# Two layers of attention and experts on one core: the first and last steps of attention prepared by half quarters, between the groups of the half before

## The chip, the core and the metric

The kernel runs on one core of a Trainium2 chip. The metric is the time of one execution on the device in microseconds, and less is better. TensorE multiplies matrices and transposes; VectorE does the elementwise work, the maxima and the reductions; ScalarE does activations and copies; GpSimd (POOL in the profile) does elementwise work beside them and issues the indirect DMAs; SyncE (SP) issues most of the other DMAs. [...]

## The reference

The input `x` has 16 x 256 rows of 128 numbers in f32. All arithmetic is f32. Cut to what matters:

```python
x = L0_attn_a_x                                    # (16, 256, 128)
x = x + attn_a(layernorm(x))    # 16 heads of 8, softmax within blocks of 64 along axis 1
x = x + ffn(layernorm(x))
x = x + attn_b(layernorm(x))    # linear, 16 heads of 8 along axis 0 (16 long), with a bias, linear
x = x + ffn(layernorm(x))

def ffn(x):                                        # 8 experts, hidden 512
    top_vals, top_idx = top_k(flat_x @ Wr, 2)
    combine = the softmax of top_vals, put at top_idx, zero elsewhere
    h = silu(flat_x Wg[e]) * (flat_x Wu[e])
    return sum over e of combine[e] * (h Wd[e]) / sqrt(12)
```

`attn_b` adds to its scores a bias that is 1 on the diagonal and beside it, around the ring of 16. The kernel computes an expert only for the rows that chose it.

## The kernel before, in words

**Tiling.** The 256 positions are cut into four quarters of 64 (`NQ`); a quarter is 1024 rows, held in the tile `xq[q]` as eight groups (`NG`) of 128 rows. `CH` is half a quarter, 512 rows. "Layer 0" is attention A and the experts behind it, "layer 1" is attention B and the experts behind that.

**Attention A** (`attention_a`, L345) takes one quarter. First comes the preparation of the whole quarter: `layernorm_t` (L249) takes the statistics of eight groups on VectorE (L253), the inverse root as a `pow` on GpSimd (`rs`, L258), normalizes on VectorE (L266) and transposes on TensorE (L270); then `queries` (L287), one matmul and four scaled copies on ScalarE (L293) for each half, and `keys` (L297), one matmul, a copy (L302) and four masked products on VectorE (L304). Then the eight groups run one after the other: values (L320), scores (L374), maxima and subtraction on VectorE (L382, L383), the exponential on ScalarE (L388), transposes (L393) with their copies (L397), the product with the values (L404), the division on VectorE (`divided`, L334), and on GpSimd the bias of the values and the addition to `xq` (L411, L412).

**Attention B** (`attention_b`, L416) does the same over the other axis, two groups at a time, with a linear map `xt` (L437) before the queries and keys. Its layernorm writes one tile `lnT` of the whole quarter, because it regroups the rows by position. Behind each group's division stand a transpose of its output (`ot`, L507) and a copy into `oT` (L508); when all eight groups are done two output products `y` (L518) are added to `xq`.

**Router** (L530), one for each quarter and layer: layernorm, logits (L544), the two largest, and the place of each row among those of its expert (L607 to L615). Then 16 indirect DMAs on GpSimd (L640), the *scatters*, put the rows, with their weight and place, into a table in DRAM that is sorted by expert. `tile_tables` works out, on VectorE, which tiles of 256 rows of one expert are full by now.

**Experts** (`experts`, L796): 39 tiles for each layer, in lists of 9, 8 and 22 that become known after the routers of quarters 1, 2 and 3. `fetch` (L797) issues on SyncE the load of a tile's 256 rows (`xin`) and three weights of 256 KB each, two tiles ahead. A *unit* is half a tile: matmuls `g` and `u` (L891), tanh on ScalarE (L896), two products on VectorE (L897, L899), and `down` (L838), the second matmuls `acc` of the unit before. Behind a tile its results are put to DRAM by two indirect DMAs on GpSimd (L864). There are 79 units for each layer (`UNITS`).

**Combine** (L913): for half a quarter, one load (`back`) on SyncE (L917), which waits for the results of all tiles that can hold rows of that quarter, and two additions on VectorE (L927). It stands ahead of attention B in layer 1, and behind everything at the end, where the sums go to the output.

**What sets the order.** The generators yield after each step, and the program's main loop (from L958) interleaves them; a tile scheduler then orders each engine's queue by the program and by buffers. A router runs in every second step of the attention of the quarter that follows (L978 to L980). `beside` (L958) spreads expert units over an attention: those of layer 0 over quarters 0 to 2 of layer 1, and 9 (`BESIDE`) of its own layer over quarter 3 of each layer. The rest of the experts run after quarter 3. `follow(put_row, before[layer] + beat)` (L647) makes each scatter wait for a recent instruction of the attention (`beat`), so that they are paced. The PSUM pool `mm` has two buffers, which transposes, queries, keys, values, outputs and `y` share; scores have two of their own, the experts three and one.

**Loads** (L147 to L173). SyncE: `x` of quarter 0, then of quarter 1, the weights of attention B, then `x` of quarters 2 and 3. ScalarE: `k_sb`, all constants in one tile of 340 KB, then biases, `wq`, `wk`, `wv`, `bv`, `wr`, and a fill of layer 0's table with zeros (`fill`, L223). The fill of layer 1's table stands on SyncE behind the router of quarter 0.

Of the kernel before, what the change touches and what calls it, by code (L numbers as in the profile page):

```python
# [10 lines left out]
F32 = mybir.dt.float32  # L11
# [4 lines left out]
ALU = mybir.AluOpType  # L16
# [94 lines left out]
def hybrid_kernel(  # L111
# [35 lines left out]
    def load_x(q):  # L147
        for s2 in range(2):
            nc.sync.dma_start(
                out=xq[q][s2 * BS : (s2 + 1) * BS],  # L150
                in_=x.rearrange("(g s) t c -> s t g c", s=2)[s2, q * BS : (q + 1) * BS],
            )

    def load(name, src, shape, engine):
        t = const.tile(shape, F32, name=name)
        engine.dma_start(out=t, in_=src)
        return t

    load_x(0)
    k_sb = load("k_sb", consts, [P, K_END], nc.scalar)  # L160
    b_sb = load("b_sb", bias, [P, 6], nc.scalar)
    wq_sb = load("wq_sb", wq, [P, P], nc.scalar)
    wk_sb = load("wk_sb", wk, [P, P], nc.scalar)
    wv_sb = load("wv_sb", wv, [P, P], nc.scalar)
    bv_bc = load("bv_bc", bv.partition_broadcast(P), [P, C], nc.scalar)
    wr_sb = load("wr_sb", wr, [P, NE], nc.scalar)
    load_x(1)
# [4 lines left out]
    load_x(2)  # L172
    load_x(3)  # L173
# [4 lines left out]
    desc = k_sb[:, K_DESC : K_DESC + NE]  # L178
# [16 lines left out]
    ones = k_sb[:, K_ONE : K_ONE + P]  # L195
    tri = k_sb[:, K_TRI : K_TRI + P]
    step = k_sb[:, K_STEP : K_STEP + NJ]
    low = k_sb[:, K_LOW : K_LOW + NE * NE].rearrange("p (a b) -> p a b", b=NE)
    pads = k_sb[:, K_PAD : K_PAD + 2 * KMAX].rearrange("p (i b) -> p i b", b=2)
    in_tile = k_sb[:, K_ROW : K_ROW + 2]  # L200
    number = k_sb[:, K_NUM : K_NUM + KMAX]
    first_row = k_sb[:, K_FIRST : K_FIRST + NE]
# [20 lines left out]
    def fill(layer, engine):  # L223
        before[layer] = [
            engine.dma_start(
                out=sorted_in[layer]
                .rearrange("(e n) r -> e (n r)", e=NE)[:, 0 : TT * RW]
                .rearrange("e (p r) -> p e r", p=P),
                in_=zero.unsqueeze(1).to_broadcast([P, NE, TT // P * RW]),
            ).ins  # L230
        ]
# [3 lines left out]
    fill(0, nc.scalar)  # L235
# [7 lines left out]
    beat, att_last = [None], [None]  # L243

# [4 lines left out]
    def layernorm_t(q, name, put, keep=None):  # L249
        stats = p2.tile([P, NG, 6], F32, tag="stats", name=f"st_{name}")  # L250
        mv = p2.tile([P, NG, 2], F32, tag="mv", name=f"mv_{name}")
        for g in range(NG):
            nc.vector.bn_stats(out=stats[:, g, :], in_=xq[q][:, g, :])  # L253
            nc.vector.bn_aggr(out=mv[:, g, :], in_=stats[:, g, :])
        veps = p2.tile([P, NG], F32, tag="veps", name=f"ve_{name}")
        nc.vector.tensor_scalar(veps, mv[:, :, 1], EPS, None, ALU.add)
        rstd = p2.tile([P, NG], F32, tag="rstd", name=f"rs_{name}")
        nc.gpsimd.tensor_tensor(rstd, veps, minus_half, ALU.pow)  # L258
        for half in range(2):
            if keep is None:  # L260
                ln = p2.tile([P, 4, C], F32, tag="ln", name=f"ln_{name}_{half}")
            pt = psum(f"lnp_{name}_{half}")
            for i in range(4):
                g = 4 * half + i
                lg = ln[:, i, :] if keep is None else keep(g)
                nc.vector.tensor_scalar(  # L266
                    lg, xq[q][:, g, :], mv[:, g, 0:1], rstd[:, g : g + 1],
                    ALU.subtract, ALU.mult,
                )
                nc.tensor.transpose(pt[:, i * P : (i + 1) * P], lg, ident)  # L270
            put(half, pt)
            yield
# [14 lines left out]
    def queries(qT, half, src, w, col, name):  # L287
        pq = psum(f"q_{name}")
        nc.tensor.matmul(pq, lhsT=w, rhs=src, start=True, stop=True)
        k = qT.shape[3]  # L290
        n = CH // k
        for r in range(4):
            nc.scalar.activation(  # L293
                qT[:, half * n : (half + 1) * n, r, :], pq.rearrange("p (a k) -> p a k", k=k),
# [3 lines left out]
    def keys(kx, cols, src, w, col, name):  # L298
# [3 lines left out]
        nc.scalar.activation(kT, pk, AF.Identity, bias=b_sb[:, col : col + 1])  # L302
        for j in range(4):
            nc.vector.tensor_scalar(kx[:, j, cols], kT, head_masks[j], None, ALU.mult)  # L304


    def spread(t, half, pt, n):
        k = P // n
        parts = CH // k
        return (  # L310
            t[:, half * parts : (half + 1) * parts],
            pt.rearrange("p (a k) -> p a k", k=k).unsqueeze(2).to_broadcast([P, parts, n, k]),
        )
# [31 lines left out]
    def attention_a(q):  # L345
        lnT = p1.tile([P, TQ // BS, 2, BS], F32, tag="src", name=f"lnA_{q}")
        qT = p1.tile([P, TQ // BS, 4, BS], F32, tag="qT", name=f"qA_{q}")
        kx = p1.tile([P, 4, TQ], F32, tag="kx", name=f"kA_{q}")
        halves = [slice(0, CH), slice(CH, 2 * CH)]

        def put(half, pt):
            nc.scalar.copy(*spread(lnT, half, pt, 2))

        yield from layernorm_t(q, f"A{q}", put)
        for half, cols in enumerate(halves):
            n = f"A{q}_{half}"
            one = lnT[:, half * NG : (half + 1) * NG, 0]
            queries(qT, half, one, wq_sb, B_Q, n)
            yield
# [674 lines left out]
```

## Time and profile before

| | |
|---|---|
| time, median of three runs | 1004.81 us (1009.39, 1004.31, 1004.81) |
| the profiled execution's own time | 1054.25 us |
| its span in the profile | 1052.2 us |
| mean granted TensorE clock in it | 0.918 |
| quarter 0 of attention A, first exponential | 32.52 us |
| layer 0's attention and last router end, experts run alone | about 334 us |
| layer 1's attention begins | about 447 us |
| layer 1's experts run alone | from about 840 us |

A duration read in the profile belongs to the profiled execution, which took longer than the timed runs. In the profile PE is TensorE's matmuls, PEld its weight loads, DVE VectorE, ACT ScalarE; busy times can overlap between engines. "x <- y" after an instruction gives what it writes and reads, by the names of the program; in the waits it is who waited for whom. The clock is the share of TensorE's full speed that was granted.

### The profile page before, as it was taken

How to read it: one execution, taken by the hardware profiler on the slowest of the kernel's cores; microseconds unless marked ns; L12 is line 12 of the kernel's file. 1: busy time of each engine (PE TensorE's matmuls, PEld its weight loads, DVE VectorE, ACT ScalarE, POOL GpSimd, SP SyncE). 2: the span in 40 equal slices, each digit the busy share in tenths (PEclk: the TensorE clock that was granted, in tenths of full speed). 3: DMA queues.
4: the chain of work that ended last, by engine and by line, in shares of the span. 5: the costliest groups of instructions: out<-in, count | busy, mean ns of one | idle time of the engine just before them, and what ended most of it. 6: DMA issues, size and time to landing. Idle time of an engine off the chain costs nothing.

```text
span 1052.2 us, 17668 instructions
## 1 busy us (share of the span) xinstructions
PE 880.4 (84%) x5992; PEld 718.8 (68%) x5992; DVE 613.8 (58%) x1725; ACT 399.7 (38%) x773; POOL 363.2 (35%) x444
## 2 busy tenths in 40 slices
PE   3897788979988999969888869982888889998983
PEld 1775666858877788837767648761577677887873
DVE  4656566547656645577557546644575774556452
ACT  3334243344342334344463344331534333443331
POOL 2121550540553653340114431433034365333332
PEclk9987897869998999998998998995799999999997
DMA  8000000040323666631212302314013366668673
GB/s 201 1 1 1 29 14 1 27 122 1 105 73 109 185 187 191 197 125 41 82 41 64 110 30 81 105 34 145 1 59 105 91 196 189 184 188 256 211 217 93
DMA packets 104746, 107.69 MB, mean 102 GB/s; under 512 B 10640, under 2 KB 80016, under 8 KB 104656
## 3 DMA queue, kind: packets, MB, share of 16 engines
q1 hardware_dynamic: 93520, 85.97, 28.0%
q0 software_dynamic: 9088, 18.89, 5.1%
q10 hardware_dynamic: 2048, 1.70, 0.6%
q8 instruction: 48, 0.79, 0.3%
q14 instruction: 42, 0.34, 0.1%
HBM read 83.38 MB, written 23.13 MB: 101 GB/s over the span
## 4 chain that ended last, share of the span: by engine, by line
PE 67%; DVE 11%; DMA 6%; ACT 6%; POOL 5%; issue 3%; another core or an unknown queue 1%; SPq 1%; ACTq 0%; POOLq 0%; DVEq 0%
PE g L891 11%; PE acc L841 11%; PE u L891 10%; PE o_A L404 5%; PE sc_A L374 4%; PE t_A L393 3%; PE sc_B L460 3%; PE v_B L320 3%; PE o_B L495 3%; DMA back<-results 2%; PE v_A L320 2%; PE lg_F L544 2%; DMA results<-yo,to 2%; PE y L852 2%; PE xt L833 1%
## 5 line engine op out<-in xcount | busy, mean ns | idle before, releaser
L864 POOL DMA_INDIRECT results<-yo,to x156 | 153.6, 984 | 275.1 <-ACT yo L857 246.0
L640 POOL DMA_INDIRECT sorted_in<-rows,pos_i_F x128 | 125.0, 977 | 142.8 <-DVE att_B L339 28.5
L841 PE MATMUL acc<-h,w 128*128 128x256 f32 x624 | 167.6, 386 | 6.3 <-DVE h L899 6.1
L891 PE MATMUL u<-xT,w 128*128 128x256 f32 x624 | 166.7, 387 | 6.5 <-DVE th L897 5.8
L891 PE MATMUL g<-xT,w 128*128 128x256 f32 x624 | 166.1, 386 | 3.1 <-ACT xT L835 1.2
L896 ACT ACTIVATE th<-g 128x512 f32<-128x512 f32 x156 | 93.3, 598 | 174.6 <-PE g L891 92.1
L897 DVE SCALAR_TENSOR_TENSOR th<-th,g 128x512 f32<-128x512 f32 x156 | 106.2, 682 | 69.3 <-ACT th L896 48.7
L841 PEld LDWEIGHTS acc<-h,w 128*128 128x128 f32 x624 | 115.3, 192 | 26.0 <-DVE h L899 10.9
L891 PEld LDWEIGHTS g<-xT,w 128*128 128x128 f32 x624 | 116.2, 192 | 20.5 <-ACT xT L835 3.4
L891 PEld LDWEIGHTS u<-xT,w 128*128 128x128 f32 x624 | 112.6, 192 | 20.3 <-DVE th L897 5.5
L899 DVE TENSOR_TENSOR h<-th,u 128x512 f32<-128x512 f32 x156 | 106.5, 683 | 24.1 <-PE u L891 9.8
L374 PE MATMUL sc_A<-kA,qA 128*128 128x256 f32 x256 | 74.0, 411 | 14.6 <-DVE ex_A L383 6.9
L404 PEld LDWEIGHTS o_A<-va,eT_A 128*64 128x64 f32 x1024 | 60.8, 146 | 13.3 <-ACT eT_A L397 9.8
L404 PE MATMUL o_A<-va,eT_A 128*64 128x18 f32 x1024 | 64.4, 219 | 2.1 <-ACT eT_A L397 2.1
L849 ACT COPY yT<-acc 128x256 f32<-128x256 f32 x78 | 29.1, 373 | 94.2 <-PE acc L841 73.5
L374 PEld LDWEIGHTS sc_A<-kA,qA 128*128 128x128 f32 x256 | 47.0, 204 | 24.9 <-issue 10.0
L857 ACT ACTIVATE yo<-y,xin 128x128 f32<-128x128 f32 x156 | 48.5, 365 | 40.5 <-PE y L852 34.2
L397 ACT COPY eT_A<-t_A 128x512 f32<-128x512 f32 x64 | 35.4, 588 | 70.4 <-PE t_A L393 64.4
L411 POOL TENSOR_TENSOR att_A<-att_A,bv_bc 128x128 f32<-128x128 f32 x32 | 14.7, 458 | 136.2 <-DVE att_A L339 131.8
L382 DVE TENSOR_REDUCE mx_A<-sc_A 128x8 f32<-128x512 f32 x64 | 43.8, 686 | 17.0 <-PE sc_A L374 16.1
L388 ACT ACTIVATE ex_A<-ex_A 128x1024 f32<-128x1024 f32 x32 | 33.9, 1058 | 43.4 <-DVE ex_A L383 39.9
L393 PE MATMUL t_A<-k_sb,ex_A 128*128 128x128 f32 x256 | 40.5, 307 | 7.0 <-issue 2.6
(173 smaller groups left out, 1319.6 us busy)
## 6 DMA issues: line engine op xcount, KB each, us to landing
w<-in_wg SPq DMA_DIRECT2D x78, 256.0 KB
w<-in_wu SPq DMA_DIRECT2D x78, 256.0 KB
w<-in_wd SPq DMA_DIRECT2D x78, 256.0 KB
xin<-sorted_in SPq DMA_DIRECT2D x78, 132.0 KB
back<-results SPq DMA_DIRECT2D x16, 512.0 KB
results<-yo,to POOLq DMA_INDIRECT x156
xq<-in_x SPq DMA_DIRECT2D x8, 256.0 KB
sorted_in<-rows,pos_i_F POOLq DMA_INDIRECT x128
```

The source lines that it names most:

```text
L320: nc.tensor.matmul(pv[:, a * P : (a + 1) * P], lhsT=src[:, g * n + a].rearrange("p r k -> p (r k)"), rhs=w, start=True, stop=True,)
L374: nc.tensor.matmul(sc[:, v * 4 * BS : (v + 1) * 4 * BS], lhsT=qT[:, blk, 2 * v : 2 * v + 2, :].rearrange("p r k -> p (r k)"), rhs=kx[:, :, ...
L393: nc.tensor.transpose(pt[:, i * P : (i + 1) * P], ex[:, b, 2 * i : 2 * i + 2, :].rearrange("p h k -> p (h k)"), ident,)
L404: nc.tensor.matmul(po[b * BS : (b + 1) * BS, i * 18 : (i + 1) * 18], lhsT=eT[:, b, 2 * v + i % 2, u * BS : (u + 1) * BS], rhs=vt[:, b, 2 * ...
L640: put_row = nc.gpsimd.indirect_dma_start(out=sorted_in[layer], out_offset=bass.IndirectOffsetOnAxis(ap=pos_i[:, k, g : g + 1], axis=0), in ...
L841: nc.tensor.matmul(acc[:, 0:TT], lhsT=w[:, 2, hc * P : (hc + 1) * P], rhs=h[:, j * TT : (j + 1) * TT], start=(hc == 0), stop=(hc == NHC - 1),)
L857: nc.scalar.activation(y[:, b, :], py[:, b * P : (b + 1) * P], AF.Identity, scale=t[:, b, C : C + 1],)
L864: put_row = nc.gpsimd.indirect_dma_start(out=results[layer], out_offset=bass.IndirectOffsetOnAxis(ap=to[:, b : b + 1], axis=0), in_=y[:, b ...
L891: nc.tensor.matmul(p[:, j * TT : (j + 1) * TT], lhsT=w[:, k, hs], rhs=xT, start=True, stop=True,)
L896: nc.scalar.activation(th, pg, AF.Tanh, scale=0.5)
L897: nc.vector.scalar_tensor_tensor(th, th, 1.0, pg, ALU.add, ALU.mult)
L899: beat[0] = nc.vector.tensor_tensor(h, th, pu, ALU.mult).ins
```

## The change

1. **Loads.** Only half of quarter 0 of `x` (SyncE) and five loads on ScalarE (`k_sb` cut to 100 KB, `wk`, `wq`, biases, `wv`) are issued at once. All others go on SyncE, in the order of first need, and `follow(some.ins, arrived)` makes each of them wait for the statistics of that first half. The other constants become a tile of their own, `k_late`. Both fills stand at the end of that list.
2. **`layernorm_t`** takes a list of halves and yields after the statistics and the `pow`, after the normalization, and after the transposes, each for one half. There are 16 more `ve` (VectorE) and 16 more `rs` (GpSimd) in all.
3. **Attention A** becomes `prepare_a(q, half)`, five steps up to the queries, which now come behind the keys, and `attention_a(q, half)`, four groups. Its tiles `src`, `qT`, `kx` are halves in two buffers in place of whole ones in one. The preparation of the next half is woven between the groups of the one that runs.
4. **Attention B** becomes `normal_b`, `prepare_b(q, half)`, `attention_b(q, half)` and `finish_b`. `begin_b(q)` is two combines, `normal_b` and the first `prepare_b`: 11 steps, woven into the second half of the quarter before; for quarter 0 among eight units of layer 0, and for quarter 3 among eight units of layer 1, after quarter 2 has been finished. The transpose `ot` of a group (`turn`) is done before the next group's product, and that of the last one at the half's end.
5. **The spreading.** `weave(main, n, sides)` takes the place of `beside`: it spreads any number of side generators over `n` steps. Routing is spread over the two halves (at most 15 and 30 of its steps). Beside quarter 3 stand 15 units, 7 in its first half and 8 in its second. In `router`, steps of `tile_tables` stand between the scatters, where before they stood ahead of them. The `beat` is set to the subtraction of a group's scores, its exponential and its division.

The instructions are otherwise the same, except that ScalarE issues fewer loads. The core of the diff:

```diff
-    load_x(0)
-    k_sb = load("k_sb", consts, [P, K_END], nc.scalar)
...
+    late = []
+    load_x(0, slice(0, NG // 2))
+    k_sb = load("k_sb", consts[:, 0:K_DESC], [P, K_DESC], nc.scalar)
+    wk_sb = load("wk_sb", wk, [P, P], nc.scalar)
+    wq_sb = load("wq_sb", wq, [P, P], nc.scalar)
     b_sb = load("b_sb", bias, [P, 6], nc.scalar)
...
     wv_sb = load("wv_sb", wv, [P, P], nc.scalar)
...
+    late.clear()
+    late += load_x(0, slice(NG // 2, NG))
+    bv_bc = load("bv_bc", bv.partition_broadcast(P), [P, C], nc.sync)
+    late += load_x(1, slice(0, NG))
+    k_late = load("k_late", consts[:, K_DESC:K_END], [P, K_END - K_DESC], nc.sync)
+    wr_sb = load("wr_sb", wr, [P, NE], nc.sync)
+    late += load_x(2, slice(0, NG))
+    late += load_x(3, slice(0, NG))
...
+        for half in halves:
+            gs = range(4 * half, 4 * half + 4)
+            stats = p2.tile([P, 4, 6], F32, tag="stats", name=f"st_{name}_{half}")
...
+            arrived[0] = nc.vector.tensor_scalar(veps, mv[:, some, 1], EPS, None, ALU.add).ins
+            nc.gpsimd.tensor_tensor(rstd[:, some], veps, minus_half[:, some], ALU.pow)
+            yield
...
+    def prepare_a(q, half):
...
+        yield from layernorm_t(q, [half], n, put)
+        yield from keys(kx, lnT[:, :, 0], wk_sb, B_K, n)
+        queries(qT, lnT[:, :, 0], wq_sb, B_Q, n)
+        ready[q, half] = lnT, qT, kx
+        yield
...
+                if pending is not None:
+                    turn(*pending)
                 po = psum(f"o_{n}")
...
-                att = divided(po[:, 0 : H * (D + 1)], n)
+                pending = g, divided(po[:, 0 : H * (D + 1)], n)
...
+    def weave(main, n, sides):
+        taken = [0] * len(sides)
+        for k, _ in enumerate(main):
+            for i, (side, count) in enumerate(sides):
+                while taken[i] < min(count * (k + 1) // n, count):
+                    taken[i] += 1
+                    next(side, None)
...
+    def begin_b(q):
+        for part in range(2 * q, 2 * q + 2):
+            combine(0, part)
+            yield
+        yield from normal_b(q)
+        yield from prepare_b(q, 0)
...
+    BEGIN_B = 2 + 6 + 3
...
+        if layer == 0:
+            first = prepare_a(0, 0)
+            next(first)
+            for some in late:
+                follow(some.ins, arrived)
+            run(first)
+        else:
+            weave(begin_b(0), BEGIN_B, [(units(0, FIRST), FIRST - unit[0])])
...
+            for half in range(2):
+                sides = [(routing, ROUTER // 2 if half == 0 else ROUTER)]
+                last = (q, half) == (NQ - 1, 1)
+                if layer == 0:
+                    main = attention_a(q, half)
+                    if not last:
+                        sides.append((prepare_a(q + half, 1 - half), 5))
+                else:
+                    main = attention_b(q, half)
+                    if half == 0:
+                        sides.append((prepare_b(q, 1), 3))
+                    elif q < NQ - 2:
+                        sides.append((begin_b(q + 1), BEGIN_B))
...
+                weave(main, STEPS[layer], sides)
+                if layer == 1 and half == 1:
+                    finish_b(q)
+                    if q == NQ - 2:
+                        n = BEGIN_B - 3
+                        run(routing)
+                        weave(begin_b(q + 1), BEGIN_B, [(units(1, n), n)])
```

## The prediction, made before the changed kernel ran

> **What bounds the kernel now.** I read the page first (engines, slices, chain), then a table of stretches cut at the stages, then single stretches of the timeline.
>
> ```profile
> PE 880.4 (84%) x5992; PEld 718.8 (68%) x5992; DVE 613.8 (58%) x1725; ACT 399.7 (38%) x773; POOL 363.2 (35%) x444
> ...
> PE   3897788979988999969888869982888889998983
> ...
> PEclk9987897869998999998998998995799999999997
> ...
> PE 67%; DVE 11%; DMA 6%; ACT 6%; POOL 5%; issue 3%; another core or an unknown queue 1%; SPq 1%; ACTq 0%; POOLq 0%; DVEq 0%
> ```
>
> TensorE is busy 84% of the span and holds 67% of the chain, so it is the bound, but not evenly: the notches in its row (slices 0, 3, 17, 23, 27) come with notches in its granted clock. So I count, for a stretch, what TensorE lost: length minus busy time times granted clock. The columns here: stretch, length, PE, PEld, DVE, ACT, POOL busy, then clock, DMA share, GB/s.
>
> ```profile
> 0.00:32.50 32.50, 11.78 (x32) 6.52 (x32) 17.34 (x74) 10.04 (x13) 6.26 (x28) 0.95 0.69 162
> 32.50:70.00 37.50, 36.77 (x360) 32.14 (x360) 23.86 (x57) 15.77 (x22) 5.48 (x12) 0.95 0.01 1
> 70.00:97.00 27.00, 20.25 (x97) 14.08 (x98) 16.20 (x61) 11.16 (x17) 6.24 (x7) 0.68 0.00 1
> 97.00:142.00 45.00, 37.47 (x329) 31.27 (x330) 26.76 (x86) 13.96 (x21) 21.71 (x30) 0.89 0.08 25
> ...
> 447.10:486.00 38.90, 27.35 (x111) 18.00 (x110) 28.48 (x81) 16.96 (x25) 13.67 (x22) 0.87 0.28 90
> ...
> 592.00:645.20 53.20, 41.39 (x275) 30.95 (x274) 29.91 (x104) 21.69 (x36) 14.96 (x19) 0.87 0.23 75
> ...
> 708.50:759.90 51.40, 26.01 (x105) 17.22 (x106) 23.84 (x92) 15.76 (x23) 10.01 (x15) 0.63 0.25 77
> ```
>
> Losses so worked out, from these rows and the same view's other rows: start 32.5 - 11.78 x 0.95 = 21.3 us; the starts of quarters 1, 2, 3 of layer 0 13.2 + 10.5 + 12.9 = 36.6; the routing stretches behind two of them 11.7 + 11.8 = 23.5; the router of quarter 3 (307.5 to 334) 9.1; in layer 1 the four quarter starts 15.1 + 6.1 + 17.2 + 35.0 = 73.4 and the groups between them 3.3 + 7.9 + 9.8 + 5.8 = 26.8. Groups that run undisturbed lose little (32.5 to 70: 37.5 - 36.77 x 0.95 = 2.6). The expert stretches lose 3.7 from 334 to 447; the end, from 840 on, 28.7. All rows together: 231 of 1052.
>
> What a quarter's start is made of, in layer 0 (columns: start, duration, engine, line):
>
> ```profile
> 68.36 1.06 ACT L388 ACTIVATE ex_A<-ex_A 128x1024 f32<-128x1024 f32 x1 [0.41 <-DVE ex_A L383]
> ...
> 77.39 0.29 DVE L253 BATCH_NORM_STATS2 st_F<-xq 128x6 f32<-128x128 f32 x1 [1.10 <-POOL xq L412]
> ...
> 78.19 1.65 POOL L258 TENSOR_TENSOR rs_F<-ve_F,minus_half 128x8 f32<-128x8 f32 x1 [0.83 <-DVE ve_A L256]
> ...
> 79.87 2.14 DVE L266 TENSOR_SCALAR rows<-xq,mv_F,rs_F 128x128 f32<-128x128 f32 x8 [1.69 <-POOL rs_F L258]
> ...
> 88.33 2.79 ACT L293 ACTIVATE qA<-q_A,q_bias,q_scale 128x512 f32<-128x512 f32 x4 [0.71 <-PE q_A L289]
> ...
> 96.85 1.06 ACT L388 ACTIVATE ex_A<-ex_A 128x1024 f32<-128x1024 f32 x1 [5.15 <-DVE ex_A L383]
> ```
>
> The exponentials of two groups that follow each other are 28.5 us apart here; inside quarter 0 they are 5.05 apart. In between run layernorm, queries, keys and the first part of the router of the quarter before, in a chain through all engines. And two rows of the waits (who, for whom, us, times, longest):
>
> ```profile
> DVE st_F L253 <- POOL xq L412: 20.8, 14, 4.6
> ...
> PE ot_B L507 <- DVE att_B L339: 17.9, 14, 2.4
> ```
>
> The first is the router's statistics, which stand in VectorE's queue ahead of softmax work and wait for GpSimd's residual add, itself queued among the scatters. The second is layer 1's transpose waiting for its own group's division.
>
> [...] from 715.72 to 749.84, after an idle stretch, the clock is 0.50 throughout. [...] before, eight issues on ScalarE took 0.3 to 0.65 us each.
>
> **The change, part by part.** Durations are from the profiled execution (1054.25 us, span 1052.2), which is 4.9% over the median of the runs, 1004.81. I sum against 1054.25 and scale the gain by 1004.81/1054.25 = 0.953.
>
> *Start.* Before, the first exponential began at 32.5: the 512 KB of quarter 0 landed at 7.4, and its normalization (15.5) stood behind the statistics of quarter 1. After, 256 KB and a shorter constant block come first; I estimate their statistics done at 6.5 to 7. But the other loads now wait for those statistics, and in VectorE's new order the second half's statistics (its load issued only then) stand ahead of the first half's normalization, and quarter 1's statistics and normalization ahead of the first keys. From the statistics: issue and landing 3.5, statistics 1.8, quarter 1's load 3 more, its statistics 1.8, `pow` on GpSimd 1.65, normalization 1.1, keys 1.7, scores, maxima, subtractions 3, so about 17: the first exponential near 24.5. That is 8 us of wall, but some 5.6 of the work done by 32.5 is only deferred: gain 2. The two zero fills, `wr_sb`, `bv_bc` and the late constants move on SyncE behind the loads of x; the first scatter is at 111.7, so nothing waits for the fills. Cost zero; without that cover some 5 us each (1056 KB at 201 GB/s).
>
> *Layer 0, boundaries.* Layernorm, transposes and keys leave the boundary: in the new order they stand between groups. The queries do not; they come after the last group's output. So at each of the six boundaries without expert work a restart remains: queries 0.85, four query copies 2.8, scores 0.4, two maxima and two subtractions 4 x 0.69 = 2.75, exponential 1.06: 7.9. It was one per quarter and becomes two. Beside it stand 3.3 of TensorE work (queries, values, eight score matmuls): 4.6 lost. But VectorE's order puts ahead of these maxima: division, the last statistics (after two GpSimd adds of 0.46), one or two `pow` of 1.65, four or eight normalizations: some 7.4 from the last output, then 2.75 + 1.06 = 11.2, less 3.3: 8. [...] 9.5 each, 57 for six, against 36.6 before: -20. The bounds: 4.6 (29 in all) and 15 (90).
>
> *Routing stretches.* 23.5 before; scatters (16 of about 0.97 plus 0.3 issue) now start later, spread over 30 steps, and the statistics that waited for them fall largely into the boundary priced above. I leave 8: +15. Bounds 2 and 20.
>
> *Quarter 3 and its router.* Expert units beside it go from 9 to 15 (the difference is only moved), its own middle boundary is filled by them: -3; its router's chain has a unit every other step: 9.1 to 4, +5. Extra instructions (16 `ve`, 16 `rs`) are 0.17 on VectorE and 1.65 on GpSimd, 26 us on an engine that is 35% busy: free where no normalization waits for it, counted above where one does. Layer 0 in sum: 2 - 20 + 15 - 3 + 5 = -1.
>
> *Layer 1, quarter starts.* The first gets eight units of layer 0 beside it (before: none until 486): 15.1 to 5. The last, 708.5 to 759.9, gets eight units of layer 1: their weights and rows were already being fetched at 708.6 to 713.5, ahead of the combine's loads on SyncE, in both orders. VectorE runs one pair of units, then waits for `back` (10.6 us from the last `y` to the add at 722.5), while TensorE has some 7 us of queued unit work; then all eight (2.8 each, 22 us) cover the chain to the queries: 35.0 to 9. The two in the middle go into the second half before. Restarts: seven, each queries 0.85 + 2.8 + 0.4 + 4.1 + 1.06 = 9.2, beside values 1.8, scores 2.2 and one to two units: 3.2 lost, 22. So 73.4 becomes 5 + 9 + 22 = 36: +37. *Within groups,* the transpose is deferred by one group: most of the 17.9 goes; late next is the copy of `t_B`: 26.8 to 18, +9. *Combine loads* of quarters 1 and 2 are added in VectorE's order before the attention that runs: -4 where its load is late. Layer 1: +42.
>
> Sum: -1 + 42 = 41, times 0.953 = 39: 1004.81 - 39 = 966.
>
> **The rivals.** (a) *Only the query chain counts:* VectorE's waits for GpSimd at the six boundaries hide behind the queries. For it: 7.9 and 7.4 overlap partly. Then 4.6 + 1.5 each: 20 more, and a filled transition another 10: 71 x 0.953 = 68: 937. (b) *Little:* the eight units do not cover 708 to 760, because VectorE's wait for `back` holds `h` and so the gate buffers; 12 lost again, and 12 more where the A boundaries cost 11.5: 17 left, 16 scaled: 989. (c) *Slower: half clock behind every boundary.* Before, a quarter's start was followed by long half-clock runs (70.6 to 87.6 stood at 0.50). If each of 13 boundaries draws some 13 us of it, dense work there costs 6.5, 5 more than priced: 65, so 24 x 0.953 slower: 1028. It decides from 41/13 = 3.2 us more per boundary. Against it: 36.5 to 70.5, right behind the first restart, is at 1.00. (d) *The order undoes it:* the instructions do stand interleaved in the built program, so that the change does nothing is out; no case.
>
> **How the numbers follow.** My case (950 to 985): 0.55. (a) 0.20, (b) 0.14, within 0.5% (1000 to 1010, about what a measurement of this kernel can tell from no change) 0.04, (c) 0.07. Faster 0.89, same 0.04, slower 0.07. The range leaves out the far ends of (a) and (c): 930 to 998.
>
> **What would show it.** The profile after: the first exponential near 24.5; gaps between the exponentials of about 15 us at each boundary of quarters 0 to 2 (5 from group to group, not 28); `st_F` or `rows` waiting for GpSimd just before them; TensorE at 8 or 9 in the slices around 710 to 750 before; the `ot_B` wait near zero; a mean clock above 0.918. Wrong I am if layer 0 shortens by over 15 us, if slices behind boundaries stay near half clock, or if the fill around quarter 3 of layer 1 stays empty.

## The result, and the profile after

1002.81 us in the median of 20 executions, against 1010.83 of 20 beside them: 0.9926 of the time before, 95% interval 0.99 to 0.9951. The forecast was 966, with a range of 930 to 998. The profiled execution after took 1007.37 us (span 1005.3), 47 us under the one before, nearly what the steps said (41). But the timed kernels differ by 8 us. The likely reason is that the two profiles came from different chips: as the first experiments show, the kernel before takes about 1011 us on one chip and 1050 to 1060 on four others. The chip of these two profiles themselves is not on record.

The page after (engines, slices, granted clock, chain):

```profile
PE 880.1 (88%) x5992; PEld 723.8 (72%) x5992; DVE 623.4 (62%) x1741; ACT 395.9 (39%) x773; POOL 371.3 (37%) x460
...
PE   3988698888999999989987989797988999998993
...
PEclk9998776798999999999978699799999999999997
...
PE 65%; DVE 13%; DMA 6%; ACT 5%; POOL 5%; issue 4%; SPq 1%; ACTq 0%; POOLq 0%; DVEq 0%
```

The notch of 2 in slice 27 is gone, and but for the first and the last slice none is under 6. The clock is lowest in slices 4 to 7 (0.6 to 0.7), where the routers of quarters 0 and 1 run, and in 20 to 22 (0.6 to 0.8), of which 21 and 22 have the first router of layer 1 (its statistics begin at 540.8). The table of stretches, cut at the first exponential of each half (columns as before: PE, PEld, DVE, ACT, POOL busy, clock, DMA share, GB/s):

```profile
0.00:24.60 24.60, 7.87 (x22) 4.53 (x23) 13.38 (x57) 5.78 (x8) 6.07 (x29) 1.00 0.77 189
24.60:52.20 27.60, 23.85 (x218) 19.19 (x217) 18.10 (x45) 12.92 (x19) 4.65 (x9) 1.00 0.08 24
52.20:82.80 30.60, 24.10 (x218) 19.09 (x217) 21.64 (x65) 12.80 (x19) 6.73 (x11) 1.00 0.01 2
82.80:125.20 42.40, 34.48 (x246) 28.33 (x245) 23.90 (x79) 14.45 (x22) 12.57 (x18) 0.78 0.03 11
...
671.80:731.70 59.90, 51.84 (x395) 41.47 (x394) 41.45 (x114) 24.84 (x49) 27.31 (x33) 1.00 0.43 133
731.70:768.20 36.50, 29.07 (x268) 23.01 (x267) 24.27 (x90) 15.22 (x27) 10.11 (x11) 0.91 0.11 33
```

The first exponential is at 24.6 (forecast 24.5). The start of quarter 3 of layer 1 (671.8 to 731.7) loses 8.1. A half without routing loses 3.8 or 6.5, one with it 42.4 - 34.48 x 0.78 = 15.5. And 731.7 to 768.2, the first half of quarter 3, loses 10.0, where a restart of 3.2 was forecast.

One boundary of attention A, from the timeline (start, duration, engine):

```profile
67.06 1.07 ACT L410 ACTIVATE ex_A<-ex_A 128x1024 f32<-128x1024 f32 x1
...
74.76 2.78 ACT L313 ACTIVATE q_A<-q_A,q_bias,q_scale 128x512 f32<-128x512 f32 x4 [2.25 <-PE q_A L311]
...
75.38 0.29 DVE L268 BATCH_NORM_STATS2 st_F<-xq 128x6 f32<-128x128 f32 x1 [1.10 <-POOL xq L435]
...
77.42 1.11 DVE L279 TENSOR_SCALAR rows<-xq,mv_F,rs_F 128x128 f32<-128x128 f32 x4 [1.06 <-POOL rs_F L273]
...
78.45 1.83 DVE L279 TENSOR_SCALAR ln_A<-xq,mv_A,rs_A 128x128 f32<-128x128 f32 x4
...
80.20 1.27 DVE L404 TENSOR_REDUCE mx_A<-sc_A 128x8 f32<-128x512 f32 x2
...
82.77 1.06 ACT L410 ACTIVATE ex_A<-ex_A 128x1024 f32<-128x1024 f32 x1 [5.23 <-DVE ex_A L405]
```

15.7 us from exponential to exponential (forecast about 15), with the queries last and two normalizations ahead of the maxima, as the order had said. This boundary was read rightly. Of the six between quarters 0 and 3, three are so (13.7, 15.7 and 16.6 us); the other three, with more of the routing beside them, take 19.9 to 22.9. One of these:

```profile
102.28 1.06 ACT L410 ACTIVATE ex_A<-ex_A 128x1024 f32<-128x1024 f32 x1 [0.43 <-DVE ex_A L405]
...
125.19 1.06 ACT L410 ACTIVATE ex_A<-ex_A 128x1024 f32<-128x1024 f32 x1 [4.77 <-DVE ex_A L405]
```

### The profile page after: what moved, and what is told of

Its sections match the earlier page's. It is cut to its first block, busy times and chain, and to the rows that moved or that the text cites. A ratio compares the mean times of both kernels' runs of the same rounds, so it can differ in the third digit from the quotient of the medians.

```text
span 1005.3 us, 17682 instructions
## 1 busy us (share of the span) xinstructions
PE 880.1 (88%) x5992; PEld 723.8 (72%) x5992; DVE 623.4 (62%) x1741; ACT 395.9 (39%) x773; POOL 371.3 (37%) x460
## 4 chain that ended last, share of the span: by engine, by line
PE 65%; DVE 13%; DMA 6%; ACT 5%; POOL 5%; issue 4%; SPq 1%; ACTq 0%; POOLq 0%; DVEq 0%
PE g L933 11%; PE u L933 10%; PE acc L883 10%; PE o_A L426 5%; PE sc_A L396 4%; PE v_B L339 4%; PE o_B L540 3%; PE t_A L415 3%; PE sc_B L503 2%; DMA back<-results 2%; DMA results<-yo,to 2%; PE t_B L527 2%; DMA xin<-sorted_in 2%; PE lg_F L585 2%; POOL sorted_in L680 2%
## 5 line engine op out<-in xcount | busy, mean ns | idle before, releaser
L933 PE MATMUL u<-xT,w 128*128 128x256 f32 x624 | 163.8, 384 | 5.4 <-DVE th L939 5.2
L396 PE MATMUL sc_A<-k_A,q_A 128*128 128x256 f32 x256 | 81.5, 448 | 27.7 <-DVE ex_A L405 18.4
L396 PEld LDWEIGHTS sc_A<-k_A,q_A 128*128 128x128 f32 x256 | 51.7, 223 | 41.2 <-issue 21.3
L419 ACT COPY eT_A<-t_A 128x512 f32<-128x512 f32 x64 | 36.0, 587 | 45.6 <-PE t_A L415 45.4
L404 DVE TENSOR_REDUCE mx_A<-sc_A 128x8 f32<-128x512 f32 x64 | 43.2, 684 | 14.9 <-PE sc_A L396 14.6
L410 ACT ACTIVATE ex_A<-ex_A 128x1024 f32<-128x1024 f32 x32 | 33.9, 1059 | 38.4 <-DVE ex_A L405 32.0
L415 PEld LDWEIGHTS t_A<-k_sb,ex_A 128*128 128x128 f32 x256 | 34.4, 159 | 18.2 <-ACT ex_A L410 6.7
```

The costliest lines, as they stand in the source:

```text
L396: nc.tensor.matmul(sc[:, v * 4 * BS : (v + 1) * 4 * BS], lhsT=qT[:, blk, 2 * v : 2 * v + 2, :].rearrange("p r k -> p (r k)"), rhs=kx[:, :, ...
L404: nc.vector.tensor_reduce(mx[:, 0:8], sc3, AX.X, ALU.max)
L415: nc.tensor.transpose(pt[:, i * P : (i + 1) * P], ex[:, b, 2 * i : 2 * i + 2, :].rearrange("p h k -> p (h k)"), ident,)
L933: nc.tensor.matmul(p[:, j * TT : (j + 1) * TT], lhsT=w[:, k, hs], rhs=xT, start=True, stop=True,)
```

## The experiments

The runs fell on five chips. The kernel before took 1011 us on chip 6, and 1053, 1062, 1062 and 1060 on chips 8, 11, 3 and 0 (the slow chips, below). Each ratio is to the kernel before on the same chip, with its 95% interval in brackets. Each chip was used in one session only, so these runs cannot tell the chip from its session.

**The kernel before and the changed one, again.** No edit.

> The kernel before, unchanged, to get a second profile of it. The profile that the prediction was made from took 1054 us, the twenty timed executions 1004 to 1018. Theory P (that one profiled execution was not typical, and the 44 us that it has over the median sit in a few places rather than everywhere): this profile's span is 1000 to 1020, TensorE idles about 40 us less than there, and the stretch around the start of quarter 3 of layer 1 (51.4 us long, 0.63 clock) is much shorter or at a higher clock. Theory U (the excess is uniform, as the scaling by 0.953 took it): every stretch is about 4% shorter, and the losses of the quarter starts in layer 1 still sum to about 70 us.

Chip 8: ratio 0.9992 (0.9955 to 1.0029), span 1048.0, within 5 us of the shown profile, which is thus typical of a chip like this one. P and U both fall: the span is not 1000 to 1020, and the stretches are as long as in the shown profile, to within a few us each.

> The kernel before once more, for its profile on the same chip as the three others here. If this is a chip on which it takes about 1010 us, Theory C expects 40 us less lost in layer 1 than in the profile shown (where its losses were 145 us from the last exponential of attention A on), and the same in layer 0. If it takes 1050, it repeats the profile shown within 5 us in every stage.

> The changed kernel, unchanged, beside the kernel before on one chip, to have both profiles from the same chip: on chip 8 the kernel before took 1052 us in the median of 51 executions, while it took 1011 in the twenty timed beside the changed kernel. Theory C (the two profiles of before and after came from different chips, so that 42 of the 47 us between them are the chip and not the change): on one chip the ratio is 0.99 to 1.0 and the stages of layer 1 in which expert units stand among attention show nearly equal losses. Theory A (the effects of the two layers add): layer 0 alone cost 27 us and layer 1 alone gave nothing on chip 8, so there this is 1.02 to 1.03.

> The changed kernel as the reference for the three others, on the same chip. On chip 6 and in the first measurement it stood at 0.994 and 0.993 to the kernel before; from the parts on chips 8 and 11, where the kernel before itself takes 1053 and 1062 us, Theory C2 (the slow chips lose more in the changed kernel's fuller stretches) expects 1.0 to 1.015 if this is such a chip, and 0.992 to 0.997 if it is one like chip 6.

Before on chip 6: 1013.55 (one execution), span 1011.6. Cut as in the table below, its losses are some 15 us less than in the shown profile up to the last exponential of attention A and some 17 us less behind it, not 40 in layer 1 alone. After: 0.9944 (0.992 to 0.9967) on chip 6, **1.0186 (1.0127 to 1.0245) on chip 3**: slower there. The ratio that C expects holds, but not its equal losses in layer 1; C2 has the sign, and its 1.015 is too low. Theory A was not tried as it stands, on chip 8. The change's sign differs between the two chips.

**One layer alone.** The other layer gets the main loop, the attention and the router of the kernel before. For layer 0 alone:

```diff
         else:
-            weave(begin_b(0), BEGIN_B, [(units(0, FIRST), FIRST - unit[0])])
+            old_1()
+            continue
```

> The change in the loads and in layer 0 alone (attention A by halves, routing spread, 15 units beside quarter 3 there); layer 1 runs whole quarters, with the kernel before's order, transposes and 9 units. The prediction's steps give layer 0 about 1 us: ratio 0.995 to 1.005. A rival, from the two profiles (last exponential of attention A at 307.5 before and 327.0 after, with six more units of 2.8 us done): 3 us slower, 1.000 to 1.006. If layer 0 carries the whole measured gain: 0.990 to 0.994.

> The change in layer 1 alone (attention B by halves, begin_b among units, deferred transpose, 15 units beside quarter 3 there); loads and layer 0 as in the kernel before. The prediction's +42 us would give a ratio of 0.96. Theory P: most of that was lost only in the one profiled execution, so this gives the measured gain and no more: 0.985 to 0.995. If the two layers work against each other, this is under 0.985 and layer 0 alone over 1.005.

Chip 8: layer 0 alone 1.0262 (1.0218 to 1.0307), layer 1 alone 0.9995 (0.996 to 1.0031). All three expectations for layer 0 miss: it costs 26 us on such a chip. Of layer 1's forecast 42 us hardly any are there: the medians are 3 apart, and the interval takes in no change. Both profiles of layer 1 are from this chip: first start, the rest of attention B, and what stands behind its last exponential; before,

```profile
446.30:479.80 33.50, 21.57 (x88) 13.50 (x88) 27.09 (x79) 14.97 (x20) 12.49 (x21) 0.90 0.23 76
479.80:801.80 322.00, 258.83 (x2220) 205.66 (x2219) 192.23 (x560) 124.51 (x221) 95.23 (x106) 0.89 0.22 69
801.80:1048.00 246.20, 214.41 (x1105) 181.31 (x1104) 129.63 (x287) 88.42 (x222) 92.88 (x95) 0.97 0.59 179
```

and with layer 1 changed:

```profile
449.50:488.00 38.50, 35.30 (x185) 28.47 (x184) 34.25 (x96) 17.48 (x34) 21.17 (x29) 1.00 0.59 187
488.00:799.90 311.90, 255.72 (x2175) 202.97 (x2174) 189.69 (x557) 124.85 (x221) 95.45 (x107) 0.91 0.21 65
799.90:1042.90 243.00, 208.26 (x1061) 177.13 (x1059) 125.92 (x281) 83.27 (x208) 90.44 (x93) 0.94 0.57 172
```

The first start loses 3.2 in place of 14.1, as forecast (5). The middle loses 79.2 in place of 91.6 (79.9 and 88.7 when it is cut by halves), where 53 was forecast. Behind the last exponential 9 more are lost, where no change was forecast.

**No units at two starts of layer 1.**

```diff
-    FIRST = BEGIN[0] + BEGIN_B - 3
+    FIRST = BEGIN[0]
-            weave(begin_b(0), BEGIN_B, [(units(0, FIRST), FIRST - unit[0])])
+            run(begin_b(0))
...
-                        weave(begin_b(q + 1), BEGIN_B, [(units(1, n), n)])
+                        run(begin_b(q + 1))
```

> The changed kernel without expert units beside the first and the last start of a quarter in layer 1: the eight of layer 0 are spread over quarters 0 to 2 and the eight of layer 1 over quarter 3, where the kernel before had them too. The prediction's terms (10 us at the first start, 26 at the last) make this 36 us slower than the changed kernel: a ratio of 1.025 to 1.035. Theory F (units are a filler of fixed amount, so that what they cover at a start they uncover among the groups: 44 us won at two starts, 37 lost in other halves): within 10 us of the changed kernel, 0.985 to 1.005, with the losses back at the starts and gone from the first halves of quarters 1 to 3.

> Without units beside the first and the last start of a quarter in layer 1, now with the changed kernel on the same chip. The prediction's terms: 36 us over the changed kernel. Theory F: at most 10 us over it.

Chip 11: 1.0171 (1.0122 to 1.022). Chip 3, beside the changed kernel: 1.0198 (1.0141 to 1.0254), medians 1082.05 against 1078.79. So 3 us, give or take some 9 by the two intervals, and not 36: Theory F's size. (F's ratio of at most 1.005 misses: it took the changed kernel to be at 0.993, which it is not on these chips.) The table of stretches of the changed kernel on chip 3, for the first start, the boundary into quarter 1, and the start of quarter 3 with the half ahead of it:

```profile
469.80:507.50 37.70, 34.39 (x175) 27.73 (x174) 34.24 (x96) 16.87 (x33) 20.55 (x29) 0.95 0.56 174
535.30:575.00 39.70, 31.31 (x270) 25.15 (x270) 23.75 (x64) 15.31 (x25) 4.33 (x4) 0.85 0.17 54
713.30:781.30 68.00, 57.23 (x395) 45.76 (x395) 41.64 (x115) 25.13 (x48) 27.84 (x33) 0.90 0.38 117
```

and without units at the starts:

```profile
469.60:496.30 26.70, 19.98 (x91) 13.83 (x90) 23.28 (x73) 10.27 (x16) 11.10 (x17) 0.81 0.33 103
525.20:563.10 37.90, 33.67 (x312) 27.23 (x310) 23.19 (x64) 18.13 (x32) 5.90 (x6) 1.00 0.20 65
710.20:771.80 61.60, 37.91 (x284) 28.33 (x284) 32.16 (x96) 17.51 (x29) 21.81 (x27) 0.75 0.25 78
```

Losses go from 5.0 to 10.5 and from 16.5 to 33.2 at the starts, 22 in all, and from 13.1 to 4.2 at the boundary that has units again. In the first halves of quarters 1 to 3 they hardly move (23.0 to 21.0, 12.8 to 14.9, 9.3 to 6.7), so of the places in which F looks for what the two covers cost elsewhere, one is seen, with 9 us; where the rest comes back is not shown. These two profiles also lie 13 us apart (1070.3 and 1083.7), further than the medians; taken by them alone, the covers would be worth 13, still not 36.

**The transpose.** Two edits that mirror each other: the transpose at once in the changed kernel (shown), and deferred, alone, in the kernel before.

```diff
-                pending = g, divided(po[:, 0 : H * (D + 1)], n)
+                att = divided(po[:, 0 : H * (D + 1)], n)
                 beat[0] = att_last[0]
                 yield
+                turn(g, att)
```

> The changed kernel with the transpose of a group's output right behind its own division, as in the kernel before. The prediction's term for it: 9 us slower than the changed kernel, 1.0 to 1.005. Rival (the deferred transpose waits less for VectorE, but nothing waits for it): no difference, 0.99 to 0.996.

> The transpose of a group's output right behind its own division, now with the changed kernel on the same chip. The prediction's term: 9 us over the changed kernel. Rival of no difference: within 3 us. From chip 11 alone (1.0208 to the kernel before, where the variant with a later router stood at 1.0069) it may be more: 10 to 15 us.

> The kernel before with one part of the change alone: the transpose of a group's output in attention B done before the next group's product, not right behind its own division. The prediction's term for it is 9 us, and undoing it in the changed kernel cost 11: ratio 0.989 to 0.993. Rival (in the kernel before, expert units stand among the groups and fill that wait; the halves, whose groups have fewer units, needed it more): 0.997 to 1.002.

1.0208 (1.0157 to 1.026) on chip 11, where the changed kernel was not run, so that this ratio decides nothing; 1.0283 (1.0229 to 1.0336) on chip 3, medians 11 us over the changed kernel. Alone in the kernel before 0.9912 (0.9874 to 0.9949) on chip 0: 9.3 us. The term of 9 was right, and the rivals of no difference fall.

**Preparation a group earlier, router later.**

```diff
-                        sides.append((prepare_a(q + half, 1 - half), 5))
+                        sides.append((prepare_a(q + half, 1 - half), 5, 0, 18))
...
-                        sides.append((prepare_b(q, 1), 3))
+                        sides.append((prepare_b(q, 1), 3, 0, 14))
...
-                        sides.append((begin_b(q + 1), BEGIN_B))
+                        sides.append((begin_b(q + 1), BEGIN_B, 0, 15))
...
-                sides = [(routing, ROUTER // 2 if half == 0 else ROUTER)]
+                sides = [(routing, ROUTER // 2, 6, STEPS[layer]) if half == 0 else (routing, ROUTER)]
```

The two new numbers are the main steps between which `weave` spreads a side. The first run has the first and the last of these pieces, the second all four, and the two parts the first three and the last.

> The changed kernel with the preparation of the next half of attention A ended one group earlier (five steps spread over the first 18 of 24, so that the queries stand ahead of the last group's values) and with the router's first step delayed by one group at the start of a quarter, so that its statistics do not stand ahead of the next scores' maxima on VectorE. Theory R (what is left at each boundary of layer 0 is the restart: queries, copies, scores, maxima, exponential in a row): the exponentials stay 5 to 8 us apart over the boundaries, in place of 13.7 to 22.9, and six boundaries give 5 to 6 us each, 30 to 36 us: ratio to the kernel before 0.955 to 0.965. Theory G (GpSimd's pow and scatters or the clock hold the boundary): at most 10 us, 0.98 to 0.993.

> The changed kernel with the preparation ended one group earlier in both layers and the router's start one group later in each quarter: the preparation of attention B's second half over the first 14 of 20 steps, that of the next quarter over the first 15. Theory R (the restarts of layer 1, too, are what is left): another 10 us under the variant that does this for attention A alone, 0.97 to 0.98. Theory U (in layer 1 units fill the restarts, and what is lost there is the units' own waits): no gain over that variant, 0.985 to 0.995.

> The variant with early preparation and late router in both layers, beside its extension on the same chip. On a chip where the kernel before takes about 1010 us: 0.948 to 0.955 as there. On one where it takes 1050 or more: 0.965 to 0.98, from early preparation alone at 0.98 on chip 11.

> Half of the better variant (0.9505): the changed kernel with the preparation ended one group earlier in both layers, and the router's start as in the changed kernel. Theory R1 (what is left at a boundary is the chain from the queries through ScalarE to the next scores): most of the 45 us come from this half, 0.955 to 0.97. Theory R2 (it is the router's statistics, which wait for GpSimd in VectorE's queue ahead of the next maxima): little, 0.985 to 0.994.

> The other half: the router's first step delayed by six steps of the quarter's first half, the preparation as in the changed kernel. R1: little, 0.98 to 0.994. R2: most, 0.955 to 0.97. If each alone gives little and both together 45 us (a chain in parallel with another, so that only both shorten the boundary), both are 0.98 to 0.994.

Early preparation in layer 0 only, with the router late in both: 0.9908 (0.9881 to 0.9934), chip 8. This lies in Theory G's range and not in R's, but both ranges took the changed kernel to be at 0.993. It was not run on chip 8; an estimate from its two layers alone there (1.0262 and 0.9995) puts it at 1.026, some 37 us above, which is R's size (30 to 36 us) and not G's (at most 10). Both layers: **0.9505 (0.9481 to 0.9528), 960.25 us, on chip 6**, and 0.9762 (0.9721 to 0.9802) on chip 0. The first is under all that was expected, the second in the range for such a chip. Preparation only: 0.98 (0.9754 to 0.9845), router only: 1.0069 (1.0045 to 1.0093), both chip 11. Both miss the ranges written for them, which again took a chip like 6. The changed kernel was not run on chip 11. If it stands there as on chip 3, at 1.0186, the preparation alone wins 39 thousandths and the router alone 12, by this estimate: most of the gain is the preparation's (R1). On chip 6, by the cut of the table below, quarters 0 to 2 of attention A lose 41.3 in place of 62.7, and the rest of attention B 45.6 in place of 59.2. The boundary into quarter 1 with both, on chip 6:

```profile
65.15 1.06 ACT L410 ACTIVATE ex_A<-ex_A 128x1024 f32<-128x1024 f32 x1
...
69.51 0.78 ACT L313 ACTIVATE q_A<-q_A,q_bias,q_scale 128x512 f32<-128x512 f32 x1
...
70.94 1.11 PE L426 MATMUL o_A<-va,eT_A 128*64 128x18 f32 x16
...
72.72 0.69 DVE L404 TENSOR_REDUCE mx_A<-sc_A 128x8 f32<-128x512 f32 x1 [1.58 <-PE sc_A L396]
...
77.10 1.06 ACT L410 ACTIVATE ex_A<-ex_A 128x1024 f32<-128x1024 f32 x1 [5.46 <-DVE ex_A L405]
```

The queries are copied before the last output is multiplied, and the next maxima start 7.6 us behind the last exponential, in place of 13.1 above. From exponential to exponential it is still 12.0 us (15.7 above), and 11.9 to 19.1 at five of the six boundaries, not R's 5 to 8: the queries' chain was a good part of what was left there, but not all of it. The preparation moved as a whole, so that its queries were not tried apart from its other steps.

The last variant adds to early preparation and late router a delay of two steps for the router's rank matmuls, and shares the units of quarter 3 of layer 1 between its halves:

```diff
         yield
+        yield
+        yield
         pr = psum(f"rank_{n}")
...
-                    goal = BESIDE * (1 + half) // 2
-                    goal = max(goal, unit[layer])
+                    goal = unit[layer] + (BESIDE - unit[layer]) // (2 - half)
```

> The variant with early preparation and late router in both layers (0.9505 on chip 6), and two things more: the rank matmuls of the router two steps later, since TensorE waited 3.5 us for them at the head of its queue, behind a copy on GpSimd that stands behind its pow; and the units left for quarter 3 of layer 1 shared between its two halves (11 by the end of the first, where it had none). If both waits count: 6 to 12 us under that variant, 0.94 to 0.945 on a chip like 6; if the rank's wait only moves to the scatters, 0.948 to 0.953. On a slow chip 0.96 to 0.975.

> Its extension (rank matmuls two steps later, units of quarter 3 of layer 1 shared between its halves), on the same chip. If the two waits count: 6 to 12 us under the variant without them. If they only move: within 4 us of it.

0.9694 (0.9643 to 0.9746) on chip 3 and 0.9751 (0.9709 to 0.9794) on chip 0, there 2 us under the variant without it, which is inside the noise of the two: as in the second expectation, these two waits only move.

## Why the prediction was wrong

Losses by stage, length minus busy time times clock, in us. Forecast: by the prediction's steps, from the profile shown. On chip 6 both are whole kernels. On chip 8 each stage is before against the run in which that stage's layer alone is changed. On chip 3 only the changed kernel has a profile.

| stage | forecast | chip 6 | chip 8, that layer alone | chip 3, after |
|---|---|---|---|---|
| start | 21.3 to 19.3 | 19.9 to 16.6 | 19.9 to 16.4 | 15.5 |
| A, quarters 0 to 2 | 62.7 to 67.7 | 52.0 to 62.7 | 60.5 to 75.4 | 70.4 |
| A, quarter 3 and its router | 11.1 to 9.1 | 10.8 to 5.4 | 8.4 to 8.6 | 8.7 |
| experts alone | 3.7 to 3.7 | 0.3 to 0.0 | 4.7 to 11.4 | 12.4 |
| first start of B | 15.1 to 5 | 17.2 to 5.3 | 14.1 to 3.2 | 5.0 |
| the rest of B | 85.1 to 53 | 71.1 to 59.2 | 88.7 to 79.9 | 87.6 |
| behind the last exponential | 28.7 (from 840) | 34.3 to 36.2 | 38.2 to 47.2 | 49.0 |

The measure is not exact. On chip 6 the table shows 20.4 won, the spans 11.3. The same product taken in slices of 1 us shows 15.8 won, and the rest of B then goes from 67.0 to 59.9. The readings below keep their direction in either cut.

**Right:** the first exponential; the first start of B; the boundary shown; the transpose, whose wait for VectorE fell from 17.9 to 1.3 us.

**Near by luck:** the sum of losses after (190 forecast, 185.2 on chip 6), and layer 0 on chip 6 (its first three rows lose 2 there, forecast 1). The parts were wrong both ways: halves with a boundary but without routing lost 3.8 and 7.2 on chip 6, where the boundary alone was put at 9.5 (8, and 1.5 for a lower clock, an estimate of the author's that is not shown here: the clock in these two halves was 1.00 and 0.97); and "I leave 8" for the routing stretches was some 30 (16.1 + 11.0 + 15.4 + 9.2 in quarters 1 and 2, less four boundaries of 5.5). On chip 8 the layer alone cost 26 us.

**The step that failed:** "Layer 1, quarter starts ... So 73.4 becomes 5 + 9 + 22 = 36: +37." With the transpose and the combines the rest of B was to win 32. It won 12 on chip 6 and 9 on chip 8, where the transpose alone wins 9 to 11 (measured on chips 0 and 3). On chip 6, 14 of the missing 20 were not there to be won (71.1 before, for 85.1), and 6 are new losses (59.2 after, for 53). On chip 8, where before is as it was priced, all that is missing is on the side of after: 79.9 for 53, and 9 more behind the last exponential. The starts did fall. The same view on chip 6, before (483 to 626 are quarters 0 and 1, 657.2 to 757.3 the start and first half of quarter 3):

```profile
483.00:543.60 60.60, 53.23 (x471) 41.38 (x470) 38.06 (x110) 28.96 (x49) 9.62 (x10) 1.00 0.18 53
543.60:553.00 9.40, 8.90 (x108) 7.85 (x106) 7.25 (x14) 5.17 (x10) 6.03 (x7) 0.84 0.24 67
553.00:626.10 73.10, 59.74 (x457) 45.11 (x454) 40.40 (x125) 29.37 (x51) 25.90 (x31) 0.84 0.26 79
...
657.20:730.90 73.70, 45.79 (x340) 33.70 (x338) 37.09 (x118) 26.19 (x45) 21.62 (x27) 0.77 0.23 75
730.90:757.30 26.40, 26.28 (x272) 22.93 (x271) 23.74 (x77) 10.32 (x21) 9.20 (x9) 1.00 0.18 57
```

and after:

```profile
508.40:548.20 39.80, 31.33 (x269) 24.79 (x270) 23.53 (x65) 15.24 (x24) 4.33 (x4) 0.83 0.17 54
548.20:588.70 40.50, 34.36 (x290) 27.71 (x289) 26.39 (x90) 16.24 (x29) 20.07 (x26) 0.83 0.17 51
588.70:626.10 37.40, 33.26 (x304) 26.24 (x302) 22.79 (x64) 18.24 (x33) 13.22 (x14) 1.00 0.28 89
...
665.80:726.20 60.40, 53.34 (x395) 42.53 (x395) 41.49 (x115) 24.84 (x48) 27.36 (x33) 0.97 0.43 132
726.20:762.80 36.60, 29.17 (x268) 23.15 (x267) 24.22 (x90) 15.27 (x27) 10.21 (x11) 0.91 0.10 33
```

With the halves ahead of them, the starts of quarters 2 and 3 lose 4.1 in place of 22.9 and 8.7 in place of 38.4. But the start of quarter 1 loses 13.8 in place of 7.4, and the first halves of quarters 1 and 3 12.0 and 10.1 in place of 1.9 and 0.1 (quarter 2: 9.0, was 0.3). The forecast took the cover of eight units as new. It is moved: quarters 0 to 2 have 19 units where they had 27, and the first half of quarter 3 has none, because its goal, `max(7, 8)`, is met by the eight begun before (the 7 and 8 told of under the change hold for layer 0 only). The run without them puts the two covers at 3 us, not 36. The rest is the restart in each half, which the forecast saw, but at 3.2 us each in layer 1: the first halves of quarters 1 to 3, with a restart and few or no units beside it, lose 9.0 to 12.0 here, and ending the preparation earlier, with a later router, took back 13.6 of the rest of B's losses on chip 6.

**The frame.** "Times 0.953" treated the profile's 49 us over the median as spread over everything. Against chip 6's profile of the same kernel its span is 40.6 us longer, and 32 of these are losses: 237.7 by this cut in the shown profile, 205.6 on chip 6. A gain that is priced in such losses is not there on a chip that does not have them. The time that it was taken from, 1004.81, was also 6 us under the median of twenty. **A reading** was also off: of the five notches that were to come with notches in the clock, slices 3 and 27 have them; the clock's row has a 9 in slices 0, 17 and 23. And six boundaries at 4.6 are 28, not 29; nothing rests on that.

**The rivals.** (a) was further off than the forecast. (b) fails: the eight units did cover the start. (c) fails on chip 6, where the mean clock rose from 0.919 to 0.933. On chip 3 the kernel did become slower and the mean clock of the executions fell from 0.915 to 0.904, but not by half clock at boundaries alone: by the table it loses more on chip 3 than on chip 6 in the stages with boundaries (70.4 for 62.7 in A, 87.6 for 59.2 in B), in the experts (12.4 for 0.0) and at the end (49.0 for 36.2; see the last section). The case of no change was nearest in number, by luck: gains and losses cancel, and much changed.

## To carry to other kernels

Filler work is a fixed amount: where a change lays it over a gap, charge the place it leaves (two covers priced at 36 us were worth 3 here, on chip 3). When a pipeline is cut into more pieces, charge a restart for every cut: the first halves of quarters 1 to 3 of layer 1, with one each, lost 9.0 to 12.0 us on chip 6, and ending the next piece's preparation one group earlier, with a later router, won 46 us over the changed kernel there. And a profile that takes 5% longer than the timed runs may be another chip's: take one from the chip that is timed before pricing a change in it.

## What the runs showed of the hardware

The kernel before took 1011 us on chip 6 and 4 to 5% more, 1053 to 1062, on the four others. Yet undisturbed expert units take the same on chips 6 and 3 (six in 16.9 us), and so does the changed kernel's stretch behind the last exponential of attention A (24.7 us, clock 1.00). Among the expert units the largest excess stands where GpSimd issues scatters and results back to back beside them (one every 1.27 us in the timeline below): units 24 to 29 and 102 to 107, at the end of the two last routers, take 26.5 us a six in the changed kernel on chip 3, and 16.9 on chip 6.

This goes with the change, layer by layer. On chip 8, units 24 to 29 take 25.4 us with layer 0 changed, 18.1 with layer 1 changed and 20.9 before; units 102 to 107 take 21.8, 26.8 and 19.4. An estimate from the units around them (18 to 35 and 96 to 113), before on chip 8 and after on chip 3, each against chip 6, puts some 14 us here, of the 22 to 25 by which the change does worse on chip 3 than on chip 6. Which part of a layer's change does it (the steps of `tile_tables` between the scatters are one candidate) was not tried. On chip 3, in the timeline:

```profile
384.17 1.03 PE L933 MATMUL g<-xT,w 128*128 128x256 f32 x4
...
386.95 0.96 POOL L680 DMA_INDIRECT sorted_in<-rows,pos_i_F  x1 [0.30 <-issue]
...
387.77 0.60 ACT L938 ACTIVATE th<-g 128x512 f32<-128x512 f32 x1 [4.19 <-PE g L933]
388.22 0.96 POOL L680 DMA_INDIRECT sorted_in<-rows,pos_i_F  x1 [0.30 <-issue]
...
390.78 0.37 ACT L891 COPY yT<-acc 128x256 f32<-128x256 f32 x1 [2.40 <-remote]
```

ScalarE begins 2.6 us after the matmuls that it waits for should have ended (384.17 + 1.03). The profile gives the wait as PE's; in the last line it names no more than "remote", none of the core's engines. What holds ScalarE there is not settled.
